# Two-layer graph attention on one core: row sums of three of four head groups by accumulating transfers, with the order of the work laid anew

## The chip, the cores and the metric

One Trainium2 chip, of which the kernel uses one core. The metric is the device time of one execution in microseconds (us). The engines are TensorE (PE in the profile, its weight loads PEld), VectorE (DVE), ScalarE (ACT), GpSimd (POOL) and SyncE (SP), which here only issues transfers. Each runs its own queue of instructions in order and waits on semaphores for the others.

## What is computed

32 graphs of 512 nodes with 256 features, and two layers. The first is a transformer block with 8 heads over an undirected adjacency with self loops, with two layer norms and an MLP of 1024; the second is attention over the directed adjacency. Behind each layer stands a residual and a layer norm without weights. All is float32. Cut to what matters:

```python
def _L0_gnn_ref(x, adj, Wqkv, ...):
    allowed = (adj > 0) | (jnp.swapaxes(adj, 1, 2) > 0) | eye
    q, k, v = jnp.split(x @ Wqkv.T + bqkv, 3, axis=-1)      # 8 heads of 32
    scores = jnp.einsum('bhqd,bhkd->bhqk', q * scale, k)
    attn = jax.nn.softmax(jnp.where(allowed[:, None], scores, -jnp.inf), axis=-1)
    ctx = jnp.einsum('bhqk,bhkd->bhqd', attn, v)
    x = _layernorm(x + ctx @ Wo.T + bo, ln1_g, ln1_b)
    ff = jax.nn.relu(x @ W1.T + b1) @ W2.T + b2
    return _layernorm(x + ff, ln2_g, ln2_b)

x = _layernorm(x + _L0_gnn_ref(x, adj, ...))
x = _layernorm(x + _L1_gnn_ref(x, adj, ...))   # attention alone, mask adj == 0
```

The softmax is done without a maximum: weights p = exp(score) times the mask, a context sum of p times v, and a division by the row sum of p. How the row sums are made is what the change is about.

## The kernel before, in words

**Steps.** The function `plain` has a class `Graph` with one method for each step of a graph: one instruction or a few on one engine. Arguments are mostly a layer (0 or 1) and a part. The order of all steps is written out by hand, under a manual schedule: `opening(a, b, c, d, e)` for the first graphs, `period(a, ..., e)` called 26 times with five consecutive graphs, and `closing` for the last. A step goes to the end of its engine's queue, so the text's order is each engine's order. In a period, graph b is in layer 1, c in the MLP and around it, d starts layer 0, e loads; a ends.

**Attention.** A layer has two head groups hg of four heads, and a group four blocks of 128 keys, so k from 0 to 7 stands for (hg, key block) with hg = k // 4. For each k: `scores` (L475, 8 small products into the one score tile s of four banks), `exp` (ACT, L484, s to the weights p of 128 x 4 x 512), `masked` (DVE, L488, p times mask), `product` (L495, four products into acc). `context` copies acc to cT.

**Row sums.** The weights of the four key blocks of a group are first added into one tile: `pair(layer, k)` adds p of k + 1 to p of k by an accumulating transfer on GpSimd's queue (L508, 1 MB), and `fold` adds two tiles on DVE (L511). What is left is p of number 2 + hg, whose 128 partitions are to be summed too. There are two ways. `sums` (L519) does it on PE: four products with a block of ones, into a PSUM bank psR. Groups in `SPREAD` do without: `halve` (L535) adds the upper 64 partitions to the lower 64, and again 32 to 32, by accumulating transfers on GpSimd's queue, and four `spread` steps (L540, SP) copy the last 32 partitions into a tile `part`, one head each. Then DVE finishes: `blocks` (L560, transpose of 32 x 32 blocks), `reduce` (for a spread group a sum over 32, L564), `invert` (L569), `widen` (L577), `divide` (L581, cT times the inverse). `project` (PE, psO) needs both groups' divides. `guard` (GpSimd, L573) only adds the sums and inverses into a check value, and `root` (GpSimd, L610 and L611) makes the inverse deviation of a layer norm by a power.

**Direct cases.** Graph 0 in layer 0 and graph 31 in layer 1 stand at the two ends of the program; there `sums` takes all four tiles of a group one by one (`direct`).

**Wide and narrow.** The helper `dense` (its matmul is L162) does a product either in one matmul of 128 output partitions (`wide=True`) or in four of 32, side by side in the array.

**Buffers.** `slots` lists, in the order of first use, which of a tag's buffers each tile gets: three PSUM banks "d" for all of psV, psQK, psH, psF, psO, psR, psT, eight buffers "p" for weights, and so on. `part`, cT and the score tile have one buffer. A tile that takes a buffer waits for the last user of the one before.

**Opening.** `warm` (L326) runs products of ones on PE while the first x is loaded; `once(2)` (L381) computes a correction of the bias b1, 16 pairs of matmuls, and `once(0)` and `once(1)` fold the value bias through Wo.

Of the kernel before, what the change touches and what calls it, by code (L numbers as in the profile page):

```python
# [27 lines left out]
def kernel(ctx: ExitStack, tc: tile.TileContext, t: dict, out: bass.AP):  # L28
# [122 lines left out]
    def plain(pools: ExitStack):  # L151
# [7 lines left out]
        def dense(out, lhsT, rhs, start, stop, wide):  # L159

            for at in (slice(0, P),) if wide else [slice(j * HD, (j + 1) * HD) for j in range(HPC)]:
                nc.tensor.matmul(out[at], lhsT[:, at], rhs, start=start, stop=stop)  # L162

        SPREAD = {(0, 0), (1, 0)}
# [5 lines left out]
                "01201201010202020201212102110212101201202012020212010202102201201201201201011021021021021021102012102102102012012020"  # L170
                + "210212121020212121021021210210012121201202020121202020120120201201102020" * 13
                + "212120102112010201201202120121021101101221121221021202110210210210210120201201210120120120120120221212012012"
            ),
            "p": iter(
                "012345672103456712045673061537245024371652617403253074615261473065073142564213074"
                + "573021654162073153076245124673025073461526143076573014256421073453072165416273015073624512463072573046152614073653071425642173045073216541623071573062451246073253074615261473065073142564213074" * 2
                + "57301625465107352037416251467034273650124015673"
# [7 lines left out]
                "01010010010"  # L185
                + "101010" * 13
                + "1011101"
            ),
            "y": iter(
                "01230123012310320132013102130232131302312013010132102301"  # L190
                + "303012032130131302312013010132102301" * 8
                + "2003213012300303012301231010210213023102"
            ),
            "z": iter(
                "010101101001"
                + "01101001" * 13
                + "011010100101"
            ),
            "st": iter(
                "01230132013201320132103213021302132013201203"  # L200
                + "12032103210321031230213021302130" * 13
                + "1203123021032103032103210321032103213021032103213201"
            ),
            "r": iter(
                "0123102101"
                + "31102001" * 13
                + "32212010123110"
# [7 lines left out]
                "01011001"  # L215
                + "1001" * 13
                + "1001"
            ),
            "total": iter(
                "01101"  # L220
                + "1001" * 13
                + "1000101"
# [7 lines left out]
        class Graph:  # L230
# [17 lines left out]
            def bank(self, kind, n, shape):  # L248

                key = (kind, n)  # L250
                if key not in self.tiles:
                    name = f"ps{kind}_{self.b}" + "".join(f"_{i}" for i in n)
                    self.tiles[key] = ps_d.tile([P, *shape], F32, tag=f"d_{next(slots['d'])}", name=name, bufs=1)
                return self.tiles[key]

# [66 lines left out]
            def warm(self):  # L322

                ps = self.bank("W", (0,), [N])
                for _ in range(4):
# [3 lines left out]
                        ones[:, 0:1].to_broadcast([P, N]),  # L329
# [39 lines left out]
            def once(self, i):  # L369
# [9 lines left out]
                for f in range(NF):  # L379
# [133 lines left out]
            def sums(self, layer, hg):  # L513

                ps = self.bank("R", (layer, hg), [N])
                folded = [2 + hg] if not self.direct(layer) else range(hg * NQ, (hg + 1) * NQ)
# [141 lines left out]
        def opening(a, b, c, d, e):  # L658

            a.load()  # L660
            a.constants(0, 4)
            a.warm()
            b.flip(1)
            a.transpose(0, 0)
            a.transpose(0, 1)
            a.transpose_out(0, 0)
            a.cast(first[0])
            a.constants(22, 23)
            a.transpose_out(0, 1)
            a.query_key(0, 1, 0, None, wide=True)  # L670
            a.query_key(0, 0, 0, None, wide=True)
            a.query_key_out(0, 1, 0, None)
            a.query_key_out(0, 0, 0, None)
            a.scores(0, 2)
            a.exp(0, 2)
            a.entries()
            a.value(0, 1)
            a.scores(0, 1)
            a.exp(0, 1)
            a.query_key(0, 0, 1, None)  # L680
            a.query_key_out(0, 0, 1, None)
            a.entry(2)
            a.scores(0, 0)
            a.entry(0)
            a.exp(0, 0)
            a.entry(1)
            a.value(0, 0)
            a.entry(3)
            a.constants(6, 8)
            b.cast(first[6])  # L690
            a.value_out(0, 0)
            b.sort(1, 0, 0)
            a.masks(0)
            a.masks(1)
            a.scores(0, 3)
            a.query_key(0, 1, 1, None)
            a.masks(2)
            a.masked(0, 0)
            b.flip(0)
            a.masked(0, 2)  # L700
            a.constants(4, 6)
            b.sort(1, 0, 1)
            a.masked(0, 1)
            b.sort(1, 1, 0)
            a.exp(0, 3)
            a.masked(0, 3)
            a.query_key_out(0, 1, 1, None)
            a.scores(0, 4)
            b.sort(0, 0, 0)
            a.value_out(0, 1)  # L710
            a.exp(0, 4)
            a.masked(0, 4)
            b.sort(0, 1, 0)
            a.scores(0, 5)
            a.exp(0, 5)
            a.once(2)
            a.scores(0, 6)
            b.sort(0, 1, 1)
            a.masked(0, 5)
            a.exp(0, 6)  # L720
            a.product(0, 0)
            a.product(0, 1)
            a.product(0, 2)
            a.scores(0, 7)
            b.sort(1, 1, 1)
            a.exp(0, 7)
            b.sort(0, 0, 1)
            b.join(0, 0)
# [2241 lines left out]
```

## Time and profile before

| what | value |
| --- | --- |
| median of 3 runs | 2994.34 us (2994.19 to 2996.27) |
| the profiled execution | 2996.1 us, its span 2994.3 us |
| mean clock granted to TensorE | 0.996 |
| PE row sums, L519, x624 | 79.8 us busy |
| DVE masking, L488, x512 | 1162.5 us busy, 2278 ns each |
| DVE folds, L511, x186 | 424.1 us busy, 2281 ns each |
| GpSimd pairs, L508, x186 | 171.3 us busy, 7.8 us from issue to landing (median) |
| GpSimd halvings, L535, x124 | 106.9 us busy; 512 KB land after 5.9 us, 256 KB after 6.3 (medians) |
| SP copies into part, L540, x248 | 64 KB each, 2.0 us to landing (median) |

A line of a group reads: line, engine, operation, output <- input, shapes, count; then busy time, mean time of one in ns, idle time of the engine just ahead of it, and who ended that idle time. The busy times are of one profiled execution. PE's matmuls overlap each other, so what one step costs there is the distance from its start to the next step's start, not its duration. A float32 matmul counts as two instructions.

### The profile page before, as it was taken

The page shows a single profiled execution, that of the slowest core. Times are in us where ns is not written, and L with a number is a line of the kernel's source. Part 1 is how long each engine was busy: PE and PEld are TensorE (multiplying, and loading weights), DVE is VectorE, ACT ScalarE, POOL GpSimd, SP SyncE. Part 2 cuts the span into 40 slices and gives each one's busy share as a digit, 9 for nine tenths or more (in the row PEclk, how much of TensorE's full clock was granted, in tenths as well). Part 3 has the DMA queues.
Part 4 walks back from the last instruction along what each step waited for, and adds up shares of the span by engine and source line. Part 5 has one row for each costly group of instructions (what it writes and reads, how often), then busy time and mean ns, then how long its engine had stood idle before and what let it go on. Part 6 is the DMA issues. An engine that isn't in the chain of part 4 may idle for free.

```text
span 2994.3 us, 83802 instructions
## 1 busy us (share of the span) xinstructions
PE 2968.1 (99%) x36842; PEld 1371.5 (46%) x36842; DVE 2700.5 (90%) x3585; ACT 1747.3 (58%) x2111; POOL 998.8 (33%) x1247
## 2 busy tenths in 40 slices
PE   9999999999999999999999999999999999999997
PEld 3444444454444544444544445444444444454443
DVE  4889999999999999999999999999999999998996
ACT  4555665556656556655566565566555665655554
POOL 0333333323333323333233333233332333333332
PEclk9999999999999999999999999999999999999999
DMA  7566767767667766666676677666766766667550
GB/s 151 115 123 135 139 134 132 132 128 146 130 133 134 131 132 138 134 133 127 130 147 130 133 135 131 132 137 135 133 122 133 145 132 133 137 122 141 100 111 27
DMA packets 276436, 387.08 MB, mean 129 GB/s; under 512 B 153248, under 2 KB 237344, under 8 KB 245792
## 3 DMA queue, kind: packets, MB, share of 16 engines
q0 software_dynamic: 35744, 260.59, 47.2%
q1 hardware_dynamic: 240320, 121.05, 18.4%
q8 instruction: 291, 4.77, 0.6%
q14 instruction: 81, 0.66, 0.1%
HBM read 72.23 MB, written 33.55 MB: 35 GB/s over the span
## 4 chain that ended last, share of the span: by engine, by line
PE 96%; DVE 2%; ACT 1%; DMA 0%; issue 0%; POOL 0%; SPq 0%; DVEq 0%; POOLq 0%
PE s L475 18%; PE acc L495 15%; PE psH L162 15%; PE psF L162 14%; PE psQK_None L162 11%; PE psV L162 7%; PE psO L162 7%; PE psQK L162 4%; PE psT L436 2%; PE psR L519 2%; ACT p L484 1%; DMA p<-p 0%; DVE p L488 0%; DVE st L602 0%; PE psB L381 0%
## 5 line engine op out<-in xcount | busy, mean ns | idle before, releaser
L484 ACT ACTIVATE p<-s 128x2048 f32<-128x2048 f32 x512 | 963.4, 1882 | 493.4 <-PE s L475 487.9
L488 DVE TENSOR_TENSOR p<-p,m 128x2048 f32<-128x2048 f32 x512 | 1162.5, 2278 | 38.9 <-ACT p L484 35.4
L475 PE MATMUL s<-qT,kT 32*64 32x512 f32 x8192 | 572.1, 614 | 8.3 <-ACT p L484 4.5
L495 PE MATMUL acc<-p,v 128*32 128x512 f32 x4096 | 508.9, 597 | 0.0
L162 PE MATMUL psH<-xT,w_L_gnn_W 128*32 128x256 f32 (+1 forms) x6296 | 471.0, 380 | 0.0
L162 PE MATMUL psF<-w_L_gnn_W,hT 128*32 128x256 f32 (+1 forms) x6896 | 459.9, 380 | 0.0
L610 POOL TENSOR_SCALAR rs<-mv 128x2 f32<-128x2 f32 (+1 forms) x320 | 210.9, 659 | 686.6 <-DVE mv L605 668.1
L511 DVE TENSOR_TENSOR p<-p,p 128x2048 f32<-128x2048 f32 x186 | 424.1, 2281 | 4.2 <-DMA p<-p 3.0
L162 PEld LDWEIGHTS psH<-xT,w_L_gnn_W 128*32 128x32 f32 (+1 forms) x6296 | 300.3, 118 | 199.5 <-issue 54.7
L611 POOL TENSOR_TENSOR rs<-rs,neg_half 128x2 f32<-128x2 f32 (+1 forms) x320 | 374.0, 1169 | 26.7
L162 PEld LDWEIGHTS psF<-w_L_gnn_W,hT 128*32 128x32 f32 (+1 forms) x6896 | 286.6, 115 | 184.7 <-ACT hT L646 31.4
L508 POOL DMA_DIRECT2D p<-p x186 | 171.3, 921 | 497.5 <-PE acc L495 441.6
L646 ACT ACTIVATE hT<-psH,c_L_gnn_b 128x256 f32<-128x256 f32 x512 | 212.1, 474 | 193.7 <-PE psH L162 184.6
L475 PEld LDWEIGHTS s<-qT,kT 32*64 32x64 f32 x8192 | 119.4, 130 | 316.0 <-issue 111.0
L535 POOL DMA_DIRECT2D p<-p x124 | 106.9, 862 | 439.8 <-DVE mv L605 193.2
L162 PE MATMUL psQK_None<-xT,w_L_gnn_Wqkv 128*32 128x512 f32 (+1 forms) x1988 | 243.1, 594 | 0.7 <-ACT xT L441 0.7
L162 PE MATMUL psO<-w_L_gnn_Wo,cT 128*32 128x256 f32 (+1 forms) x2728 | 240.1, 380 | 1.8 <-DVE cT L581 1.8
L495 PEld LDWEIGHTS acc<-p,v 128*32 128x32 f32 x4096 | 118.9, 110 | 258.5 <-issue 193.7
L162 PEld LDWEIGHTS psO<-w_L_gnn_Wo,cT 128*32 128x32 f32 (+1 forms) x2728 | 154.5, 123 | 97.2 <-issue 43.0
L441 ACT COPY xT<-psT 128x512 f32<-128x512 f32 x130 | 76.0, 585 | 200.7 <-PE psT L436 200.7
L631 ACT ACTIVATE x<-z,ms,rs 128x256 f32<-128x256 f32 x128 | 73.1, 596 | 158.8 <-DVE ms L615 155.7
L602 DVE BATCH_NORM_STATS2 st<-y 128x6 f32<-128x256 f32 x384 | 155.0, 422 | 6.5
(79 smaller groups left out, 2876.3 us busy)
## 6 DMA issues: line engine op xcount, KB each, us to landing
p<-p POOLq DMA_DIRECT2D x186, 1024.0 KB, 7.8
p<-p POOLq DMA_DIRECT2D x62, 512.0 KB, 5.9
x<-in_x_dram SPq DMA_DIRECT2D x32, 512.0 KB, 4.2
code<-in_adj_dram POOLq DMA_DIRECT2D x32, 512.0 KB, 6.2
m<-code SPq DMA_DIRECT2D x32, 512.0 KB, 4.9
kT<-v SPq DMA_DIRECT2D x248, 64.0 KB, 4.2
p<-p POOLq DMA_DIRECT2D x62, 256.0 KB, 6.3
part<-p SPq DMA_DIRECT2D x248, 64.0 KB, 2.0
```

The source lines that it names most:

```text
L162: nc.tensor.matmul(out[at], lhsT[:, at], rhs, start=start, stop=stop)
L475: nc.tensor.matmul(s[half * P // 2 : (half + 1) * P // 2, j, :], self.kT(layer)[at, hg, key : key + P // 2], self.qT(layer)[at, hg, :], st ...
L484: nc.scalar.activation(self.p(layer, k), self.at("s", (layer, k), [HPC, N]), AF.Exp, scale=SCALE)
L488: nc.vector.tensor_tensor(p, p, m[:, k % NQ, None, :].to_broadcast([P, HPC, N]), ALU.mult)
L495: nc.tensor.matmul(acc[j * HD : (j + 1) * HD, :], self.v(layer)[:, kc, h * HD : (h + 1) * HD], self.p(layer, k)[:, j, :], start=(kc == 0), ...
L508: nc.gpsimd.dma_start(out=self.p(layer, k), in_=self.p(layer, k + 1), accum_op=ALU.add)
L511: nc.vector.tensor_tensor(self.p(layer, dst), self.p(layer, a), self.p(layer, b), ALU.add)
L535: nc.gpsimd.dma_start(out=p[:rows], in_=p[rows : 2 * rows], accum_op=ALU.add)
L602: nc.vector.bn_stats(self.at("st", (n, i), [6]), self.y(n, i))
L610: nc.gpsimd.tensor_scalar(rs, self.mv(n)[:, a:b, 1:2], EPS, None, ALU.add)
L611: nc.gpsimd.tensor_tensor(rs, rs, neg_half[:, a:b, None], ALU.pow)
L646: nc.scalar.activation(self.hT(h)[:, f, :], ps[:, f % 2, :], AF.Relu, bias=b1[:, f : f + 1])
```

## The change

A third of the four head groups, (1, 1), the second of layer 1, joins `SPREAD`. Its `sums` step goes from all graphs but the direct one; two `halve` steps, four `spread` steps and a `reduce` come in, and its `blocks` now reads `part`. Only (0, 1) is still summed on PE. In the two direct cases, pairs of tiles are now added by `pair` transfers first, except in group (1, 1), and `sums` takes every second tile (`step`). `warm` runs nine products of 128 columns in place of four of 512. `once(2)` is cut into four pieces that may stand apart. The order of `opening`, `period` and `closing` and all lists in `slots` are new, and so is which products are wide. The new lines shift the numbers by four: L581 is L585.

```diff
-        SPREAD = {(0, 0), (1, 0)}
+        SPREAD = {(0, 0), (1, 0), (1, 1)}
...
+            def step(self, layer, hg):
+
+                return 2 if (layer, hg) != (1, 1) else 1
...
-                ps = self.bank("W", (0,), [N])
-                for _ in range(4):
+                ps = self.bank("W", (0,), [P])
+                for _ in range(9):
...
-                        ones[:, 0:1].to_broadcast([P, N]),
+                        ones[:, 0:1].to_broadcast([P, P]),
...
-            def once(self, i):
+            def once(self, i, piece=0):
...
-                for f in range(NF):
+                for f in range(piece * NF // 4, (piece + 1) * NF // 4):
...
-                folded = [2 + hg] if not self.direct(layer) else range(hg * NQ, (hg + 1) * NQ)
+                folded = [2 + hg] if not self.direct(layer) else range(hg * NQ, (hg + 1) * NQ, self.step(layer, hg))
```

The order of a period, before, around the row sums of graph b in layer 1 (steps of other graphs cut):

```python
b.fold(1, 2, 2, 0)
...
b.halve(1, 0, P // 2)
...
b.product(1, 7)
...
b.fold(1, 3, 6, 7)
...
b.halve(1, 0, P // 4)
b.spread(1, 0, 2)
...
b.fold(1, 3, 3, 4)
...
b.sums(1, 1)
...
b.blocks(1, 1)
...
b.divide(1, 1)
...
b.blocks(1, 0)
...
b.divide(1, 0)
...
b.project(1, 0, wide=True)
```

And after, from the last product to the projection. All steps on PE between them are shown, and those of the other engines that the text speaks of:

```python
b.product(1, 7)
c.transpose(1, 0)
...
d.scores(0, 0)
...
b.fold(1, 3, 6, 7)
...
b.fold(1, 3, 3, 4)
...
c.hidden(0, 0)
c.hidden(0, 6)
...
b.halve(1, 1, P // 2)
d.scores(0, 1)
...
b.fold(1, 2, 2, 0)
...
b.halve(1, 1, P // 4)
b.halve(1, 0, P // 2)
...
c.hidden(0, 2)
...
c.hidden(0, 4)
...
d.scores(0, 2)
c.transpose(1, 1)
...
b.spread(1, 1, 0)
...
c.mlp(1, wide=True)
...
b.spread(1, 1, 3)
...
b.spread(1, 1, 1)
b.halve(1, 0, P // 4)
c.mlp(0, wide=True)
c.hidden(1, 6, wide=True)
...
d.scores(0, 4)
...
c.hidden(1, 0)
...
d.product(0, 0)
...
b.spread(1, 1, 2)
c.hidden(1, 4)
...
c.root(2, 0, 2)
c.hidden(1, 2)
...
b.blocks(1, 1)
c.affine(2, 1)
d.scores(0, 5)
...
d.product(0, 1)
...
b.reduce(1, 1)
...
d.product(0, 2)
b.spread(1, 0, 2)
...
c.mlp(2)
...
c.mlp(3)
d.product(0, 3)
b.invert(1, 1)
b.widen(1, 1)
...
b.spread(1, 0, 1)
...
b.divide(1, 1)
...
c.add(2, 2)
b.spread(1, 0, 0)
b.spread(1, 0, 3)
b.blocks(1, 0)
b.reduce(1, 0)
b.invert(1, 0)
d.scores(0, 6)
c.stats(2, 2)
c.add(2, 3)
b.widen(1, 0)
b.divide(1, 0)
d.pair(0, 2)
d.pair(0, 0)
...
c.transpose(2, 0)
...
b.project(1, 0, wide=True)
```

The opening of the changed kernel up to the eighth exp of graph 0, PE steps only: `warm`, both transposes of graph 0, its value and query-key products, then scores with `b.value(0, 0)`, `a.value(0, 0)`, three pieces of `once(2)`, the first products of graph 0 and `b.query_key(0, 1, 0, None)` between them; before, `once(2)` stood in one piece between two scores and the products of graph b came only behind the row sums of graph 0.

## The prediction

> **What bounds the kernel now.** I read the page first (busy times, then its chain), then the table of 100 us stretches, then the chain in order of time, then TensorE's own timeline.
>
> ```profile
> PE 2968.1 (99%) x36842; PEld 1371.5 (46%) x36842; DVE 2700.5 (90%) x3585; ACT 1747.3 (58%) x2111; POOL 998.8 (33%) x1247
> ...
> PE s L475 18%; PE acc L495 15%; PE psH L162 15%; PE psF L162 14%; PE psQK_None L162 11%; PE psV L162 7%; PE psO L162 7%; PE psQK L162 4%; PE psT L436 2%; PE psR L519 2%; ACT p L484 1%; DMA p<-p 0%; DVE p L488 0%; DVE st L602 0%; PE psB L381 0%
> ```
>
> TensorE (PE) is busy for 2968.1 of 2994.3 us, and the chain that ended last lies on it; the row sums (psR) hold 2% of that chain. By stretches (after the window come its length, then PE, PEld, DVE, ACT, POOL):
>
> ```profile
> 0.00:100.00 100.00, 94.05 (x1012) 42.37 (x1016) 55.34 (x68) 44.96 (x50) 13.15 (x22) 0.93 0.70 152
> ...
> 1500.00:1600.00 100.00, 100.00 (x1221) 45.26 (x1210) 93.02 (x119) 62.34 (x77) 39.39 (x45) 1.00 0.68 134
> ...
> 2900.00:3000.00 100.00, 77.38 (x1026) 35.80 (x1018) 64.97 (x105) 37.72 (x52) 20.86 (x36) 0.94 0.22 47
> ```
>
> From 400 to 2700 us PE has no idle time; it has some at the two ends only, and there its clock (the first number behind the busy times) is below 1. VectorE (DVE) has 93 of 100 and is next. The chain in order of time shows what one period costs, by one place that comes back in each:
>
> ```profile
> 1202.70 6.91 PE psF L162 x128
> 1294.28 6.91 PE psF L162 x128
> 1385.87 6.91 PE psF L162 x128
> ```
>
> 91.58 us each time. So in the 26 periods each us taken off PE is a us of time, as long as nobody else becomes late. What a step costs PE is read from starts in its timeline, since the durations overlap (start, duration, x instructions; each matmul is two, a transpose one):
>
> ```profile
> 1509.29 1.90 PE L162 MATMUL psQK_None<-xT,w_L_gnn_Wqkv 128*32 128x512 f32 x16
> 1511.12 1.11 PE L475 MATMUL s<-qT,kT 32*64 32x512 f32 x16
> 1512.17 1.06 PE L519 MATMUL psR<-p,ones 128*32 128x512 f32 x8
> 1513.05 1.90 PE L162 MATMUL psQK_None<-xT,w_L_gnn_Wqkv 128*32 128x512 f32 x16
> ```
>
> ```profile
> 485.63 1.91 PE L162 MATMUL psV<-w_L_gnn_Wv,xT 128*32 128x256 f32 x32
> 487.48 0.66 PE L436 MATMUL psT<-ident,x 128*128 128x128 f32 x4
> ```
>
> One row sum of four matmuls takes 1513.05 - 1512.17 = 0.88 us, scores 1.05. The psV pair takes 1.85 where the whole-width psT follows, and 1.76 where another narrow product does (1515.92 to 1517.68): a change between four 32-wide products and one of 128 costs 0.09. A change to scores costs the same 0.09.
>
> Last, the opening. PE waited 2.03 us for ScalarE, and its clock then fell to half (in the second fence, the third number from the end):
>
> ```profile
> 29.10 2.02 PE L475 MATMUL s<-qT,kT 32*64 32x512 f32 x16 [2.03 <-ACT p L484]
> ```
>
> ```profile
> 25.00:30.00 5.00, 2.16 (x28) 0.57 (x32) 5.00 (x3) 3.25 (x4) 0.52 (x1) 0.87 1.07 200
> 30.00:35.00 5.00, 5.00 (x35) 3.96 (x19) 5.00 (x4) 1.88 (x1) 0.00 (x0) 0.50 0.42 121
> 35.00:40.00 5.00, 5.00 (x31) 3.28 (x30) 2.04 (x1) 0.00 (x0) 0.00 (x0) 0.50 0.78 205
> 40.00:45.00 5.00, 5.00 (x52) 1.16 (x48) 2.29 (x1) 1.88 (x1) 0.00 (x0) 0.76 0.95 285
> ```
>
> That lost 5 x (0.13 + 0.50 + 0.50 + 0.24) = 6.9 us.
>
> **What the Trainium skill says.** (1) TensorEngine Tiling (Array Packing), Key Properties: a change of the tiling mode drains TensorE. The trace agrees: 0.09 us a change. (2) TensorE: Matmul & The Clock Gate, HAM oscillation: idle time makes the clock drop to half, and steady work brings it back. Seen above after a stretch with 43% busy. (3) DMA: Bandwidth & Descriptors, SWDGE vs HWDGE vs iDMA and its part on issuing engines: an accumulating transfer has to be issued by GpSimd, and transfers of all issuers share the same 16 engines. The trace has all accumulating ones on GpSimd's queue, and transfers that overlap others landing later: a halving (L535) lands 5.0 to 7.9 us after its issue, median 6.0, a part's copy (L540) after 1.9 to 5.9, median 2.0, a pair (L508) after 6.9 to 10.1, median 7.8 (all from 400 to 2500 us). (4) SBUF — State Buffer, SBUF: two separate sides: a VectorE operation with two SBUF inputs keeps a GpSimd one that reads SBUF waiting to its end. The trace has the power at L611 at 0.57 us, and at 2.66 where it began together with a fold (1541.96 us).
>
> **The change, part by part.**
>
> *Row sums off PE.* Group (1,1) of graphs 0 to 30 loses its sum: 31. The two direct cases sum pairs: graph 0 layer 0 goes from 8 sums to 4, graph 31 layer 1 from 8 to 6. So 78 sums (L519 x624, 8 each) become 41: 37 x 0.88 = -32.6 us.
>
> *Wide and narrow products.* Counted in PE's order of both kernels, changes between 32-wide and 128-wide go from 46 to 74 (1 to 2 in a period); those into and out of scores stay (511 to 512 each way). 28 x 0.09 = +2.5 us. Wide or narrow itself moves a step by some 0.02 either way: nothing. A period thus takes 91.58 - 0.88 + 0.09 = 90.79 us.
>
> *Opening.* Before, the warm-up ran to 6.47 us though x had landed at 4.8 (load issued at 0.74); nine short products are a bit over half of that work, so the transposes start at about 5.2: -1.3. The order now puts projections of two graphs and quarters of the b1 correction between the first scores, so that no wait of 2 us is left in sight. If the clock stays up, -6.9; if not, 0. I take half, -3.4, as the DMAs that feed these steps come in a new order.
>
> *The new chain of (1,1) and (1,0).* On GpSimd the order is both halvings of (1,1), then both of (1,0); each second one waits there for the first to land. From PE's transpose(1,0), which the affine just ahead of the folds on VectorE releases: center and two folds 0.4 + 2.2 + 2.3 = 4.9; issue 0.3; halving 6.0; wait 0.3; second halving and issue of the next 0.6; halving of (1,0) 6.0; wait 0.3; its second 6.0; SyncE's four copies 0.06 + 3 x 0.63 + 2.0 = 4.0; blocks, reduce, invert, widen, divide 0.71 + 0.69 + 0.25 + 0.71 + 0.68 = 3.0. Sum 31.4. PE has until project(1,0): 3 transposes at 0.55, 6 scores at 1.13, 8 hidden at 1.74, 4 mlp at 3.46, 4 products at 0.87 = 39.7. Cover 8.3 us. With the three halvings at 7.9 and the copies at 5.9 it is 9.6 later, 1.3 short. I take nothing for the periods.
>
> *What waits behind it.* GpSimd: root(2,0,2) stands behind the four halvings; its consumer affine(2,1) comes on VectorE only behind blocks(1,1), which wants the copies of (1,1) anyway. SyncE: four copies more, 4 x 0.63 = 2.5 us; sorts and an entry behind them feed joins and masks some six us later or more. VectorE: reduce of (1,1) is new, 0.69; blocks now reads SBUF, 697 for 716 ns. Its load goes from 0.925 x 91.6 = 84.7 (its mean share from 400 to 2600 us) to 85.4 of 90.8 us, 94%. Its tightest place: add(2,3) needs mlp(3); add, widen and divide of (1,0) then take 0.24 + 0.32 + 0.63 + 0.68 = 1.9, while PE has product, scores, transpose = 2.6. Cover 0.7, with no DMA in it: nothing, or up to 0.3 a period if it is gone.
>
> *The ends.* In the closing and in the first graphs the same sums of PE work leave 2 to 5 us less cover than a period: 3 to 6 us at the median landings, and up to 6.6 short at the slowest. Five graphs at 1.5 (between 0 and 5), and 2.5 for the direct cases, whose sums now want pairs (7.8 us) to land: +10. Bounds -2 (shorter waits than before, which had some 26 us of idle PE) and +25.
>
> Sum: -32.6 + 2.5 - 1.3 - 3.4 + 10 = -24.8 us. The profiled execution took 2996.1 with a span of 2994.3; the median of the runs shown, 2994.34, is 1.8 under it. Taken off the median: 2970 us.
>
> **Rivals.** *A, as summed*: 2970, own range 2962 to 2979. For it: PE without gaps, cover in the periods. *B, late transfers eat part*: the ends cost +25 and the clock gains nothing: -32.6 + 2.5 - 1.3 + 25 = -6.4, or 2988 at the worst; between that and A its middle is 2983. For it: pairs (0,2) and (0,0) are now issued one right behind the other, as are a second and a first halving, and share the engines. Against: the landings above contain such overlaps already. *C, more*: clock full, ends +3: -35.3, 2959. *D, slower: the halvings become the bound.* Cover 8.3 over three halvings: from 2.8 us above the median each, every us more is paid three times in each of the 26 periods, and at about 3.1 the period's gain of 0.79 is gone. At 3.3: (9.9 - 8.3) x 26 = 42, and 2970 + 42 = 3012. For it: GpSimd waits out each landing, so lateness adds up. Against: none of 91 halvings took over 7.9, 1.9 above the median. *E, no change*: VectorE, at 94%, or pair(1,4), whose buffer the next exp wants, takes the 0.8 of a period: 2992. That the sums might stay on PE is out: the order of after shows them gone.
>
> **How the numbers follow.** A 0.52, B 0.22, C 0.11, D 0.11, E 0.04. The range 2960 to 2988 holds A, B and about half of C. A difference of 0.2% (6 us) can just be told from none here. Faster: A, B and C, 0.85; same: E, 0.04; slower: D, 0.11.
>
> **What would show it.** Right: psF on the chain every 90.8 us; psR x328; PE still 100 of 100 in the middle; clock 1.00 from 25 to 45 us; halvings landing within 8. Wrong: PE waiting for cT (L585 of the changed kernel) before psO in each period (D), idle PE well over 26 us in the two ends (B), or VectorE waiting for part before its transposes.

## The result and the profile after

The changed kernel takes 3014.49 us in the median of 14 runs (2993.78 to 3031.15); the kernel before, on the same chips, 2994.35 us (2993.34 to 2997.07, 14 runs). The ratio is 1.0064, 95% interval 1.005 to 1.0078: slower by some 20 us, where 25 us less were forecast. The runs of the changed kernel lie 37 us apart, those of the kernel before 4 us. In the table of runs further below, two runs of "store earlier" and one of "entries first in the period" count as slow, over 1.5% above the fastest of their kernel; medians and ranges have them, ratios leave them out. The profiled execution of the changed kernel took 3010.43 us with a span of 3008.6 us.

The page of the changed kernel, its busy times and its chain, by engine and by line:

```profile
PE 2943.3 (98%) x36244; PEld 1369.4 (46%) x36244; DVE 2709.9 (90%) x3617; ACT 1736.6 (58%) x2111; POOL 931.3 (31%) x1315
...
PE 86%; DVE 6%; DMA 3%; SPq 1%; issue 1%; ACT 1%; POOL 1%; DVEq 0%; ACTq 0%; POOLq 0%
```

TensorE is busy for 24.8 us less (2968.1 to 2943.3). That this equals the forecast for the whole time is chance: the prediction's terms for TensorE's work and its clock alone (-32.6 + 2.5 - 1.3 - 3.4) make -34.8. A part of the difference is the clock, whose mean fell from 0.996 to 0.994, an estimated 6 us over the span. And 65.3 us of the span are without TensorE work now (3008.6 - 2943.3) instead of 26.2, and the chain, which lay on TensorE to 96%, leaves it for VectorE and for transfers. The table of stretches (window, its length, then busy PE, PEld, DVE, ACT and POOL, the granted clock, the DMA share and GB/s) says where:

```profile
0.00:100.00 100.00, 84.47 (x866) 40.89 (x870) 49.34 (x61) 43.67 (x46) 11.84 (x24) 0.98 0.86 180
200.00:300.00 100.00, 88.73 (x1096) 39.70 (x1084) 82.05 (x107) 52.28 (x61) 28.93 (x40) 0.95 0.70 121
300.00:400.00 100.00, 93.80 (x1228) 41.56 (x1220) 83.87 (x114) 53.92 (x69) 28.60 (x39) 0.97 0.77 145
1500.00:1600.00 100.00, 99.14 (x1192) 47.20 (x1184) 91.70 (x134) 57.68 (x70) 32.23 (x49) 1.00 0.77 146
2700.00:2800.00 100.00, 92.79 (x1256) 39.96 (x1248) 85.40 (x114) 54.01 (x66) 32.48 (x39) 0.97 0.77 138
```

The middle is nearly as full as before. The holes are in the first 400 us and at the beginning of the closing.

Four kinds of transfer on SyncE's queue come up from here on. An `entry` is a transposing transfer that makes a quarter of a mask from the adjacency. A `flip` is a transposing load of x for a new graph, a `sort` one of the 64 KB copies that put in order what it brought (kT<-v). The `store` writes a graph's result.

The chain in order of time (start, length, what) has both, the period and the transfers that broke the chain:

```profile
208.89 24.52 DMA p<-p
300.57 8.06 DMA v<-in_x_dram
310.06 9.70 DMA out_dram<-x
...
655.89 6.91 PE psF L162 x32
...
746.66 6.91 PE psF L162 x32
...
837.44 6.91 PE psF L162 x32
...
2710.77 9.27 DMA part<-p
```

The same piece of psF comes back every 90.77 us, where the kernel before had 91.58. A pair that landed after 24.5 us, a flip and a store after 8 to 10 us, and a copy of 64 KB after 9.3 us are among the transfers that stand on the chain besides. TensorE's own timeline gives what each cost it (start, duration, then in brackets the idle time ahead and its releaser):

```profile
66.53 3.13 PE L523 MATMUL psR<-p,ones 128*32 128x512 f32 x16 [3.73 <-DMA p<-p]
...
237.82 2.02 PE L479 MATMUL s<-qT,kT 32*64 32x512 f32 x16 [10.14 <-ACT p L488]
...
320.52 1.40 PE L440 MATMUL psT<-ident,x 128*128 128x128 f32 x4 [6.19 <-ACT x L635]
...
2724.41 1.08 PE L162 MATMUL psO<-w_L_gnn_Wo,cT 128*32 128x256 f32 x8 [6.41 <-DVE cT L585]
```

The largest is the one at 237. What moved in the 24 us ahead of it is seen in the DMA view of 202 to 226 us (busy share of the 16 engines in 40 slices, in tenths; GB/s in the same slices; then the issues with count, size and median landing):

```profile
DMA  4224999999000000998867999999999999997599
...
p<-p POOLq DMA_DIRECT2D x3, 1024.0 KB, 22.5
...
m<-code SPq DMA_TRANSPOSE x3, 22.2
```

Three pairs of graph 2 and three transposing mask transfers (entry) of graph 3 were in flight together, and both kinds took 22 us, where the steady stretch of the kernel before has 7.8 and 3.9. This is not bandwidth: from about 208 to 211.5 us hardly a packet begins (the zeros; the view counts a packet where it begins), although all three entries and two pairs wait to land. By the packet records fifteen packets of 8 KB, as the pairs have them, began from 206 us on and all ended at 212.2 only, after 4.4 to 6.1 us, where such a packet alone takes 0.63. The lack shows again at the end of that stretch (the windows view, columns as above):

```profile
225.00:230.00 5.00, 2.69 (x24) 0.58 (x24) 0.00 (x0) 0.39 (x1) 0.00 (x0) 1.00 0.75 98
230.00:235.00 5.00, 0.00 (x0) 0.00 (x0) 1.49 (x1) 0.00 (x0) 0.00 (x0) 0.59 0.06 13
235.00:240.00 5.00, 2.18 (x20) 0.54 (x24) 5.00 (x5) 1.94 (x2) 0.83 (x1) 0.50 0.59 98
```

From 230 to 235 us TensorE stands, its clock falls to 0.59 and then 0.50, and the DMA engines are busy to 6%, while two pairs still have to land (at 233.4 and 238.3 us). From 228.8 to 236.7 us fourteen packets of 8 KB follow one another, 0.61 us apart. A pair of 1 MB is 128 such packets, 8 for each of 16 engines if they are spread evenly; so this looks like one engine's share of two pairs, done last and alone. That is an estimate, as the records don't name the engine. When these two kinds were issued is in the timeline of all engines from 202.5 us:

```profile
202.88 0.94 POOL L512 DMA_DIRECT2D p<-p  x1
...
203.06 1.19 SPq L354 DMA_TRANSPOSE m<-code  x1
```

0.18 us apart, with two more entries 1.2 and 4.5 us behind the first. In the periods the same two kinds are 0.8 to 3 us apart; where one period had them 0.11 us apart (986.8 us), the pair took 14.4 and the entry 11.6 us, and that period 92.9 us.

### The profile page after: what moved, and what is told of

It is laid out like the page before. It is cut to its first block, busy times and chain, and to the rows that moved or that the text cites. A ratio compares the mean times of both kernels' runs of the same rounds, so it can differ in the third digit from the quotient of the medians.

```text
span 3008.6 us, 83311 instructions
## 1 busy us (share of the span) xinstructions
PE 2943.3 (98%) x36244; PEld 1369.4 (46%) x36244; DVE 2709.9 (90%) x3617; ACT 1736.6 (58%) x2111; POOL 931.3 (31%) x1315
## 2 busy tenths in 40 slices
DMA packets 287219, 425.84 MB, mean 142 GB/s; under 512 B 156320, under 2 KB 240416, under 8 KB 252832
## 4 chain that ended last, share of the span: by engine, by line
PE 86%; DVE 6%; DMA 3%; SPq 1%; issue 1%; ACT 1%; POOL 1%; DVEq 0%; ACTq 0%; POOLq 0%
PE s L479 16%; PE psH L162 14%; PE acc L499 13%; PE psF L162 13%; PE psQK_None L162 10%; PE psO L162 7%; PE psV L162 7%; PE psQK L162 3%; PE psT L440 2%; DVE p L492 2%; DMA p<-p 2%; DVE p L515 1%; PE psR L523 1%; ACT p L488 1%; SPq L544 0%
## 5 line engine op out<-in xcount | busy, mean ns | idle before, releaser
L479 PE MATMUL s<-qT,kT 32*64 32x512 f32 x8192 | 573.2, 614 | 17.4 <-ACT p L488 14.3
L499 PE MATMUL acc<-p,v 128*32 128x512 f32 x4096 | 521.2, 598 | 3.5 <-ACT v L456 1.4
L614 POOL TENSOR_SCALAR rs<-mv 128x2 f32<-128x2 f32 (+1 forms) x320 | 198.7, 621 | 749.5 <-DVE mv L609 722.8
L539 POOL DMA_DIRECT2D p<-p x186 | 155.5, 877 | 745.5 <-DMA p<-p 533.6
L162 PEld LDWEIGHTS psF<-w_L_gnn_W,hT 128*32 128x32 f32 (+1 forms) x5456 | 317.8, 123 | 139.0 <-ACT hT L650 12.6
L162 PEld LDWEIGHTS psH<-xT,w_L_gnn_W 128*32 128x32 f32 (+1 forms) x7376 | 273.5, 113 | 232.8 <-issue 65.3
L512 POOL DMA_DIRECT2D p<-p x192 | 174.1, 947 | 457.4 <-DVE st L606 209.3
L615 POOL TENSOR_TENSOR rs<-rs,neg_half 128x2 f32<-128x2 f32 (+1 forms) x320 | 267.3, 835 | 26.7
L162 PEld LDWEIGHTS psQK_None<-xT,w_L_gnn_Wqkv 128*32 128x32 f32 (+1 forms) x1976 | 64.6, 111 | 159.5 <-issue 137.6
L508 ACT COPY cT<-acc 128x512 f32<-128x512 f32 x128 | 75.0, 586 | 106.9 <-PE psO L162 88.6
```

The source lines that it names most:

```text
L479: nc.tensor.matmul(s[half * P // 2 : (half + 1) * P // 2, j, :], self.kT(layer)[at, hg, key : key + P // 2], self.qT(layer)[at, hg, :], st ...
L499: nc.tensor.matmul(acc[j * HD : (j + 1) * HD, :], self.v(layer)[:, kc, h * HD : (h + 1) * HD], self.p(layer, k)[:, j, :], start=(kc == 0), ...
L512: nc.gpsimd.dma_start(out=self.p(layer, k), in_=self.p(layer, k + 1), accum_op=ALU.add)
L539: nc.gpsimd.dma_start(out=p[:rows], in_=p[rows : 2 * rows], accum_op=ALU.add)
L614: nc.gpsimd.tensor_scalar(rs, self.mv(n)[:, a:b, 1:2], EPS, None, ALU.add)
L615: nc.gpsimd.tensor_tensor(rs, rs, neg_half[:, a:b, None], ALU.pow)
```

## The theories and the experiments

*T*: a transposing mask transfer and an accumulating pair that are issued at the same moment hold each other up, 15 to 25 us instead of 4 and 8; the new order of the opening puts them there. *R*: no such thing; the larger number of accumulating transfers crowds the DMA engines, or the order of the ends has too little cover whatever stands beside. *S* and *Q* are two smaller places: SyncE's queue in front of a store, and a short copy beside a pair. Ratios are to the kernel before, with their 95% intervals.

| kernel | median us (lowest to highest, runs) | ratio |
|---|---|---|
| changed | 3014.5 (2993.8 to 3031.2, 14) | 1.0064 (1.005 to 1.0078) |
| entries later | 2996.0 (2985.6 to 3009.8, 22) | 1.0003 (0.9993 to 1.0013) |
| store earlier | 3005.3 (2983.3 to 3032.6, 22) | 1.0029 (1.0011 to 1.0047) |
| pair behind copies | 3003.7 (2983.5 to 3023.9, 22) | 1.0028 (1.0011 to 1.0044) |
| entries beside a pair, each period | 3037.2 (3028.9 to 3048.8, 4) | 1.0148 (1.0124 to 1.0172) |
| graph 0 direct | 2992.4 (2981.2 to 3011.3, 22) | 1.0003 (0.9993 to 1.0014) |
| entries first in the period | 3015.5 (2984.2 to 3038.0, 6) | 1.0091 (1.0069 to 1.0114) |
| three moves | 2987.7 (2981.9 to 2999.9, 6) | 0.9978 (0.9963 to 0.9993) |
| all moves | 2978.5 (2975.8 to 2985.3, 5) | 0.9948 (0.9935 to 0.996) |
| plain entries | 2987.8 (2977.2 to 3003.2, 22) | 0.9983 (0.9972 to 0.9994) |
| plain entries beside a pair | 2989.7 (2979.1 to 2996.7, 12) | 0.9982 (0.9973 to 0.999) |
| plain and graph 0 direct | 2987.5 (2984.6 to 2991.1, 7) | 0.9974 (0.9963 to 0.9986) |
| plain and all moves | 2974.4 (2971.8 to 2981.9, 4) | 0.9939 (0.9922 to 0.9955) |

**Entries later.** Three steps moved within SyncE's queue, from beside graph 2's pairs to behind its copies:

```
             c.pair(0, 4)
-            d.entry(0)
...
-            d.entry(2)
...
-            d.entry(1)
...
             c.spread(0, 0, 3)
+            d.entry(0)
+            d.entry(2)
+            d.entry(1)
```

> The changed kernel with three steps of the opening moved on SyncE alone: graph 3's transposing mask transfers entry(0), entry(2) and entry(1) come behind spread(0,0,3) of graph 2, so that they no longer run beside graph 2's pairs. Theory T (a transposing mask transfer and an accumulating pair in flight together hold each other up, 15 to 25 us instead of 4 and 8): the three entries land within 5 us, graph 2's pairs within 9, TensorE's wait of 10.1 us at 237 and the clock drop behind it go, and the time falls by 12 to 20 us, to about 2997 to 3002 us (1.001 to 1.003 of the kernel before). Theory R (it is the number of accumulating transfers, or the order of TensorE's work in the ends that has too little cover, whatever stands beside): the pairs still land after 15 us or more or the wait turns up elsewhere, and the time stays at 1.005 to 1.008.

18 us less than the changed kernel. In its DMA view of 205 to 235 us the three pairs land as anywhere else:

```profile
p<-p POOLq DMA_DIRECT2D x3, 1024.0 KB, 9.0
```

The moved entries, issued at 241 to 244 us, landed after 3.4 to 4.0 us, and TensorE has no wait of over 1 us from 200 to 300. T holds for this place. In this execution the clash came at another one instead: at 336.7 us a pair and an entry were issued 0.26 us apart, both took 17 us, and TensorE waited 4.2 us.

**Store earlier.** One step moved within SyncE's queue:

```
             c.aggregate(2, 0)
+            a.store()
             e.flip(1)
...
             e.sort(0, 1, 0)
-            a.store()
```

> The changed kernel with one step of the opening moved on SyncE: graph 0's store comes ahead of graph 4's flips and sorts instead of behind the first of them. In the profile of the changed kernel ScalarE waited 14.9 us for that store to land, and TensorE 6.2 us behind it. Theory S (SyncE's queue order, the store standing behind a flip that waits for its landing): the store is issued before 300 us, the 6.2 us wait goes, and the time falls by 5 to 9 us (1.003 to 1.005 of the kernel before). Theory R (lack of cover in the opening's order): the norm is late for its own inputs, the wait is 4 us or more still, the time unchanged at 1.005 to 1.008. By theory T alone the wait at 237 us stays as it is.

ScalarE's norm of graph 2, first in the changed kernel, then in this one (timelines of ScalarE):

```profile
319.87 1.09 ACT L635 ACTIVATE x<-z,ms,rs 128x256 f32<-128x256 f32 x2 [14.90 <-DMA out_dram<-x]
```

```profile
316.21 1.10 ACT L635 ACTIVATE x<-z,ms,rs 128x256 f32<-128x256 f32 x2 [4.30 <-DVE ms L619]
```

The store was issued at 300.45 instead of 310.06, ScalarE no longer waits for it, TensorE's 6.2 us are gone, and from graph 2's first psF to graph 3's it is 91.6 instead of 100.8 us. S holds. The clash stayed (a pair after 25.6 us, TensorE's wait 8.3 us), and the runs lie 49 us apart; the gain of 9 us in the medians is no better known than the intervals say.

This execution lost time in the periods too: the 25 from graph 3 to graph 28 took 2286.9 us, 17.6 more than 25 x 90.77. TensorE waited for cT at 591, 689, 965 and 1605 us, for 4.4, 2.3, 2.8 and 1.4 us (TensorE's timeline, the first of them):

```profile
595.37 6.13 PE L162 MATMUL psO<-w_L_gnn_Wo,cT 128*128 128x256 f32 x16 [4.43 <-DVE cT L585]
```

In these four periods, and in no other, both flips landed after 8.3 to 10.8 us (their median is 6.5), and the 512 KB halving beside the second flip after 8.4 to 9.8 (median 7.3). The same pair of late flips stands in the one or two long periods of other profiles: 91.9 us at 1566 in the changed kernel, 95.1 in that of three moves, 96.7 with all moves, 95.2 with plain entries and graph 0 direct. No run moved the flips, so that they are the cause is likely and not shown.

**Pair behind copies.** One step moved within GpSimd's queue, in the closing:

```
             b.product(1, 0)
-            b.pair(1, 0)
...
             c.guard(0, 1, 0)
+            b.pair(1, 0)
```

> The changed kernel with one step of the closing moved on GpSimd: graph 28's pair(1,0) comes behind guard(0,1,0) of graph 29, so that it is issued after that graph's four short copies to part have landed. In the profile of the changed kernel the fourth copy landed after 9.3 us beside that pair, and TensorE waited 6.4 us for cT. Theory Q (a short copy's packets alternate with the pair's packets of 0.6 us and more on each engine): the four copies land within 3.5 us, the wait of 6.4 goes, and the time falls by 5 to 7 us (1.003 to 1.005 of the kernel before). Theory R (too little cover in the closing): the wait stays over 4 us, time 1.005 to 1.008.

TensorE's psO, which had waited 6.4 us, follows without a gap (its timeline), and the four copies land after 3.4 us in the median (DMA view of 2690 to 2725 us):

```profile
2719.62 3.66 PE L162 MATMUL psO<-w_L_gnn_Wo,cT 128*32 128x256 f32 x64
```

```profile
part<-p SPq DMA_DIRECT2D x4, 64.0 KB, 3.4
```

From graph 28's first psF to the end of TensorE's work it went from 345.0 to 338.2 us. Q holds, with 6.8 us.

**Entries beside a pair in every period.** The opening is left alone, and the clash is brought into the 26 periods:

```
-            d.entry(0)
...
-            d.entry(3)
...
-            d.entry(2)
...
             a.store()
+            d.entry(0)
+            d.entry(3)
+            d.entry(2)
```

> The changed kernel with the clash put into each of the 26 periods: entry(0), entry(3) and entry(2) of the graph that comes next stand behind the store on SyncE, so that they are issued about 1 us ahead of pair(1,4), where they stood 3 us and more ahead of pair(1,0). Theory T: in most periods the entries and the pair land after 10 to 25 us, the masks made of them come late, VectorE waits for m and TensorE behind it: 2 to 10 us a period, 50 to 250 us in all. Theory R (crowding only, no special clash): the entries land within 9 us, the pair within 10, as where a single entry met a pair in the kernel before (8.4 and 7.9 us), and the time stays within 10 us of that of the changed kernel.

Neither fits whole: 23 us more than the changed kernel, less than T's 50. In the profiled execution the 25 periods from graph 3 to graph 28 took 39.5 us more than 25 x 90.77, while the opening had no clash and was 12 us shorter than the changed kernel's. So the difference in the whole time says too little of what the clash costs, and not every period has one. In one of them (DMA view of 1540 to 1556 us), and in the one before it (1449 to 1465 us):

```profile
p<-p POOLq DMA_DIRECT2D x1, 1024.0 KB, 13.6
...
m<-code SPq DMA_TRANSPOSE x3, 13.7
```

```profile
p<-p POOLq DMA_DIRECT2D x1, 1024.0 KB, 9.5
...
m<-code SPq DMA_TRANSPOSE x3, 5.2
```

In the first the second entry was issued at 1544.62 us and pair(1,4) at 1544.57; in the other they were 0.66 us apart. Taken over the 24 periods between 400 and 2600 us: where an entry and the pair were issued within 0.1 us of each other (9 periods), entries took 13.3 to 16.7 us in 7; where they were 0.36 to 0.86 us apart (15 periods), no entry took over 12.0 and no pair over 9.7 us (the entries behind a pair still took 7.6 to 11.9). What a clash costs, the chain in order of time shows:

```profile
1102.98 6.91 PE psF L162 x32
1199.84 6.91 PE psF L162 x32
1290.61 6.91 PE psF L162 x32
```

96.86 us with a clash (its entries issued from 1172 us on), 90.77 in the period behind it. The seven periods with a clash took 94 to 99 us, none of the others over 91.5. So T is right about the mechanism and was too wide about when it strikes: not whenever the two are in flight, but when they start nearly together, and not always then. Nor does it strike with every accumulating transfer: in the changed kernel's profile eight entries were issued within 0.3 us of a 256 KB halving, and landed after 5.1 to 5.6 us, the halvings after 4.6 to 5.0.

**Plain entries.** The transfers themselves are changed, their place isn't; the transposition is left out:

```
-                nc.sync.dma_start_transpose(out=self.m1[:, i, :], in_=self.code[:, i * P : (i + 1) * P])
+                nc.sync.dma_start(out=self.m1[:, i, :], in_=self.code[i * P : (i + 1) * P, :])
```

> The changed kernel with every entry(i) as a plain copy of the same block of rows of code into the same tile, not a transposing one; the masks then hold another matrix than they should (the transposition of the adjacency is left out), the order, sizes and waits of all else are those of the changed kernel. Theory T (transposing transfers are what clashes with the accumulating pairs): no mask transfer or pair of graph 2 lands after 12 us, TensorE's 10 us wait at 237 goes, the median falls by 20 to 30 us to 2985 to 2995 (0.997 to 1.000 of the kernel before) and the run-to-run spread shrinks to under 15 us. Theory R (crowding by more accumulating transfers, transposing or not): the same landings of 15 to 25 us, 3005 to 3015 us.

27 us less than the changed kernel. The pair and the first entry are again issued 0.17 us apart (timeline of all engines from 196 us), and the DMA view of 195 to 220 us has for them:

```profile
196.54 0.94 POOL L512 DMA_DIRECT2D p<-p  x1
...
196.71 0.50 SPq L354 DMA_DIRECT2D m<-code  x1
```

```profile
p<-p POOLq DMA_DIRECT2D x3, 1024.0 KB, 10.0
...
m<-code SPq DMA_DIRECT2D x3, 128.0 KB, 9.9
```

10 instead of 22 us; the wait at 237 is gone. With the same number of accumulating transfers, the same bytes and the same moment, the clash is gone; as it is not there in every execution of the transposing kernel either (below), this one place would not decide between T and R, but the medians do, and the next run. The spread shrank from 37 to 26 us, not to the 15 expected.

A plain copy differs in more than the transposition: by the two pages the kernel has 287219 packets with transposing entries and 236019 without, 400 fewer for each of 128 entries, for the same 425.8 MB, and SyncE issues a copy in 0.50 instead of 1.19 us. Whether it is the transposing or the many small packets that clash was not told apart.

> The kernel with the entries put beside pair(1,4) in every period (3037 us, stalls of 13 to 16 us in 8 of 26 periods), now with the same plain copies in place of the transposing ones; the transposition of the adjacency is left out here too. Theory T: no stall in the periods, entries and pairs land within 10 us, every period 90.8 us, 2985 to 2997 us in all. Theory R: pairs and entries issued within 0.1 us of each other still land after 13 us or more, time above 3020 us.

The same edit in the kernel with entries beside a pair: 2989.7 instead of 3037.2 us. In five of the 25 periods between 400 and 2640 us a plain copy and pair(1,4) were issued within 0.1 us of each other, where seven of nine had clashed before; these pairs landed after 7.4 to 7.9 us and the copies after 5.1 at most. Over all 25 no pair took more than 9.2 and no copy more than 5.1. The packet records say the same of whole executions. Of the accumulating transfers' packets of 8 KB (median 0.65 us), 35 took over 2 us in the changed kernel, the slowest 6.1, and 182 with entries beside a pair. In the kernel before it was one, and in the four kernels with plain entries 2 to 6, none over 2.6. Two of those four have the changed kernel's accumulating transfers one for one, so their number alone, which is theory R, doesn't hold packets up. (The periods with entries over 13 us are the seven counted above, not the eight that this expectation speaks of.)

**Graph 0 direct.** The four pairs of the opening are taken out, and graph 0's eight tiles are summed on TensorE:

```
-                return 2 if (layer, hg) != (1, 1) else 1
+                return 2 if (layer, hg) != (1, 1) and self.b else 1
...
-            a.pair(0, 0)
...
-            a.pair(0, 2)
+            a.once(0)
+            a.sums(0, 0)
...
-            a.pair(0, 6)
-            a.once(0)
...
-            a.pair(0, 4)
-            a.sums(0, 0)
```

> The changed kernel with graph 0's first layer summed on TensorE from all eight score tiles again, as in the kernel before: its four pairs are gone, its row sums take 8 steps instead of 4 (3.5 us more of TensorE). Theory T/crowding in the opening (those four pairs stand beside weight loads and a transposing mask transfer that landed after 26 to 28 us, and TensorE waited 3.7 to 9.5 us for the pairs): the weight loads land within 10 us, the wait on a pair at 57 to 72 us goes, and the net is -2 to -7 us (1.003 to 1.0055 of the kernel before). Rival (pairs are right, the opening's idle time comes from its first scores and joins): +3 to +4 us (1.0075).

22 us less than the changed kernel, three times the most that was expected. Taken for itself this would have made the opening's pairs the culprit. The same edit over plain entries tells otherwise:

> Plain copies in place of the transposing mask transfers (the transposition of the adjacency is left out), and graph 0's sums direct without its four pairs. With plain copies alone the time was 2987.8 us, with graph 0 direct alone 2992.4. If the gain of graph 0 direct was a gain of its own (pairs that crowd with weight loads at 36 to 66 us, 3.5 us of sums paid back), this goes to 2978 to 2983 us; if that gain came only because the clash at 203 us was met at another moment, it stays at 2987 to 2992 us.

2987.5 against 2987.8 us: without transposing entries, graph 0's pairs cost what they save. With them the edit can help in two ways. In the profile with graph 0 direct, graph 2's pair and the entries were issued 0.5 us apart instead of 0.18 and landed after 12.1 and 10.9 us at most: the two parties had moved apart. And graph 0's own pairs, which are gone, stand beside entries too. TensorE waited for one of them 2.5 to 3.7 us in five profiles (the changed kernel, entries beside a pair, entries first, both plain ones that keep these pairs), but 6.9 to 11.7 in four (entries later, store earlier, pair behind copies, three moves), in which the slowest packet of 8 KB there took 6.0 to 12.1 us.

**Entries first in the period**, for the spread of the times:

> The changed kernel with SyncE's order in the period changed alone: entry(2) directly behind entry(0) and entry(3), then the whole-row mask load (entries) and the load of x, so that the last transposing transfer is issued some 1.5 to 2 us earlier ahead of pair(1,0). If the run-to-run spread of the changed kernel (2994 to 3031 us) comes from periods in which an entry and that pair are issued within about 0.2 us of each other (one such in the profile of the changed kernel, at 986.8 us, where the pair landed after 14.4 us), the median falls by 2 to 8 us and the highest times fall more; no pair in the periods lands after more than 14 us. Rival (the spread comes from the ends alone): median and spread unchanged, 1.005 to 1.008.

A miss: median and spread are those of the changed kernel, so the place of these entries in the period is not what spreads the times. That the ends alone do it, as the rival had it, does not follow: the profile of "store earlier" lost 17.6 us in its periods. (The edit is in the diff of all moves below.) Its profile helps in another way. That one execution took 2984.2 us, 31 less than its own median, and in it the pair and the first entry of the opening were issued at 203.86 and 204.04 us, 0.18 us apart as in the changed kernel, but landed like this (DMA view of 202 to 226 us):

```profile
p<-p POOLq DMA_DIRECT2D x3, 1024.0 KB, 10.5
...
m<-code SPq DMA_TRANSPOSE x3, 9.7
```

The same instructions at the same offset, once with the clash and once without. The order there is the same in five kernels, the offset 0.17 to 0.19 us: in the profiles of the changed kernel, of store earlier and of pair behind copies a pair landed after 24 to 26 us, in those of entries beside a pair and of entries first none after more than 12. So the offset alone does not decide it, it changes from one execution to the next, and it is a part of the spread.

**The moves together.** First the three of the beginning:

> The three moves of the first experiments together: graph 3's entries behind graph 2's copies, graph 0's store ahead of graph 4's flips, graph 28's pair(1,0) behind graph 29's guard. Measured alone they brought 0.6%, 0.35% and 0.36% against the changed kernel. If they are independent places, together 1.3%: 2975 to 2982 us, 0.994 to 0.996 of the kernel before. If they only shift the same loss (each merely changes the moment at which later steps meet), 2990 to 3000 us.

2987.7 us, between the two expectations. In the profiled execution a pair of graph 0 landed after 22.6 us beside an entry that took 32.5, and TensorE waited 11.7 us for it, to 72 us. Then with graph 0 direct and the period's order too, which was:

```
-            d.entries()
...
             d.entry(3)
+            d.entry(2)
+            d.entries()
+            d.load()
...
-            d.load()
-            d.entry(2)
```

> All of them: the three moves, the entries first in the period, and graph 0's sums direct. If the ends and the clashes are what the change lost, this comes near what the sum without the loss in the ends gives: 2966 to 2978 us (0.991 to 0.995 of the kernel before), TensorE idle under 40 us. If something else of the change costs (halvings, VectorE at 94%), it stays above 2985 us.

2978.5 us, 0.9948 of the kernel before: just above the expected range, and a version that beats both kernels. TensorE's idle time is 38.6 us. The last run puts plain entries into it:

> The kernel with all moves (2978.5 us), with plain copies in place of the transposing mask transfers (the transposition of the adjacency is left out). If the moves have taken every clash away, the time stays within 3 us of 2978.5 and what is left over 2970 is idle TensorE in the opening (11 us in the first 100); if clashes are left, it falls by 4 us or more, to 2974 or less.

4.1 us less, which four and five runs can't tell from none with certainty (the two intervals overlap): at most a few clashes are left in the version with all moves. To the 2970 of the prediction it is 4.4 us.

## Why the prediction was wrong

*The gain in the periods was right.* psF comes every 90.77 us (90.79 predicted), psR is x328, the middle has TensorE at 99 to 100 of 100. 26 x (91.58 - 90.77) = 21.1 us are won where no period is disturbed; in the profile three were, by 3.4 us in all. Wide and narrow changes, VectorE at 94% and the chain of four halvings took nothing from an undisturbed period: medians of 7.0 us for the 512 KB halvings, where 6.0 was reckoned, and 4.7 for the 256 KB ones. That all would land within 8 us, one of the signs of being right, did not hold; the slowest took 9.2. Rivals D and E did not come as summed, but D's sign, TensorE waiting for cT, did in single periods: four in the profile of "store earlier", one of 2.75 us in that with all moves, at 2568 us. The cover of 8.3 us is thin when flips are late beside the halvings.

*The opening.* The transposes start at 5.09 us (5.2 predicted), and the clock is 1.00 from 25 to 45 us, so that the clock's share of the sum was kept whole, not by half. But "no wait of 2 us is left in sight" failed: TensorE is busy for 84.5 of the first 100 us instead of 94.1. The 3.7 us wait for a pair is a part of it; by the run with graph 0 direct over plain entries, pairs instead of sums come out even there, where the sum had 3.5 us of gain and 2.5 of wait for both direct cases. Beside transposing entries the wait was up to 11.7 us.

*The step that failed is "The ends", +10 with bounds of -2 and +25.* That transfers would land late there was right; how late, and why, was not. The profiled spans differ by +14.3 us, the periods by -21.1 + 3.4 = -17.7, so that all outside the periods is +32.0, where the prediction's terms leave -24.8 + 26 x 0.79 = -4.3: 36 us more. By the medians, with what each run showed:

- 2970 predicted, 2974.4 with plain entries and all moves: 4.4 us left unexplained. In that profile TensorE is idle for 10.2 of the first 100 us, where the kernel before has 6.0.
- 2974.4 to 2987.8 with plain entries alone: 13.4 us for all moves together: SyncE's store behind a flip, the copies beside pair(1,0) in the closing, and orders around them. The first two showed as 6.2 and 6.4 us of TensorE's waits in the changed kernel; how the 13.4 divide is not known, as the profile of plain entries has the second (6.3 us) and not the first. The prediction had counted what waits in SyncE's queue as "sorts and an entry", without the store, and the copies at 5.9 at the slowest; beside a pair one took 9.3.
- 2987.8 to 3014.5: 26.7 us for what goes with transposing entries, and that is their clash with pairs as far as the runs tell. Nothing in the prediction had it.

The clash fell through at one sentence, that against rival B: "the landings above contain such overlaps already". They do, but of another kind. In the whole trace of the kernel before, three entries were issued within 0.3 us of a pair: at 286.58 us at the same moment, at 460.97 us 0.20 us behind, at 1101.69 us 0.13 us ahead. They landed after 6.6, 8.4 and 7.3 us, the pairs after 8.9, 7.9 and 8.9. The changed opening puts three entries in a row onto a pair. And a row of landings from one execution could not show that the same offset lands after 10 us once and after 22 the next time. B's upper bound of 25 us was therefore too low, and B, not A, was the kind of outcome that came, beyond its own end.

*What the Trainium skill says on it.* DMA: Bandwidth & Descriptors, Issuing engines are not separate DMA queues, has it that transfers of all issuers run on the same 16 engines and interleave: the 64 KB copy beside a pair (9.3 us instead of 2.0) agrees. The same page, Rules for kernel authors, says that a transposing transfer beside ordinary ones needs nothing. It says so of wrong data from transfers in flight together; as to time it can't be taken so here for accumulating ones: 22 us instead of 4 and 8.

*Open.* Why packets are held while both kinds wait isn't settled, nor what decides in which execution it happens. The flips are transposing transfers too, and were left as they are in every run. With plain entries the times still lie 26 us apart. Late flips, with long periods behind them, are seen in these kernels as well, without any packet held for over 2.6 us; so they look like another matter than the clash, and what makes them late wasn't tried.

## What to carry to other kernels

A transfer's landing time, taken from a steady stretch, holds for its neighbours there. When an order is laid anew, list for every transfer what else is issued within a microsecond of it, above all transposing transfers beside accumulating ones, and keep these apart by their place in the queues. A kernel whose runs have begun to spread tells of such a chance meeting before its profile does: compare several executions, since one may show the clash and the next not. And an edit that helps may only have moved two transfers apart; take the suspected meeting away first, then see whether the edit still helps.

## What the hardware showed that was not expected

- An entry and a 1 MB accumulating pair issued within 0.3 us of each other landed after 11 to 22 us, those behind them after up to 26, or the two after 7 to 11: which, changed from one execution to the next. Behind it stand single packets: fifteen of 8 KB were held for 4.4 to 6.1 us in the changed kernel's opening and let go together at 212.2 us, twelve likewise at 218.1 in the profile of pair behind copies. No such packet took over 2.6 us in the kernel before or in any with plain entries.
- One late packet can go with a long wait: in the profile of three moves a single one of 8 KB took 12.1 us, the pair in flight landed after 22.6, and TensorE waited 11.7.
- A 64 KB copy within SBUF, 2.0 us alone, took 9.3 us when a 1 MB accumulating pair had been issued 1 us ahead of it.
- Order alone, with the same instructions on every engine, moved the time by 18 us (entries later).
